# Two of the seven products of the gate and up units split once more, and the gate and up weight sums made in SBUF

## The chip, the cores and the metric

The kernel runs on one core of a Trainium2 chip. The metric is the device time of one execution in microseconds. The time of the kernel before is the median of three runs.

## What is computed

An RWKV layer at its first time step, followed by a gated feed-forward layer, on 2048 tokens of 512 features in float32. Only the second half is touched by the change:

```
x = x + rwkv(layernorm(x))            # time mix, channel mix: about the first 53% of the time
z = layernorm(x)
gate, up = split(z @ w_gate_up.T)     # 2048 x 512 times 512 x 4096
h = silu(gate) * up                   # 2048 x 2048
x = x + h @ w_down.T                  # 2048 x 2048 times 2048 x 512
```

## The kernel before

**Tiles.** The tokens are cut into 4 blocks (`b`) of 512. A weight of 512 x 512 is a "block" `n` of four quarters of 256 x 256: `WG + g` and `WU + g` are the four gate and four up blocks (`g` = 0 to 3).

**A unit** (`unit`, line 583) is one product of a weight block with a token block, 512 x 512 x 512, after Strassen and Winograd: seven products of quarters instead of eight. The weights' sums S1 to S4 and the activations' sums T1 to T4 are made ahead; the sums after the products are folded into the order of the accumulation. One product is 4 matmuls of 128 x 128 weights with 256 moving columns (L602). Its steps are `step1` (A11·B11, copied by ScalarE to the bank `accv`, L622), `step2` (A12·B21 on `accv`), `step6` (S2·T2, copied to `u2`, L633), `step5` (S1·T1, copied to `accx`, L637) and, put off into the next unit through the list `held`, `step7` (S3·T3), `step3` (S4·B22 on `accx`) and `step4` (A22·T4). `sink(i, j, c)` takes each finished quarter: `ffn_gate` (L1162) applies Silu on ScalarE, `ffn_up` (L1174) multiplies on VectorE (`tt`, L431).

**The down products** (`down_product`, L1273) already split a second time: seven products of 256 wide operands, each of seven products of 128 x 128 x 128 quarters over four chunks (L1342). ScalarE keeps intermediate results (`keep`, L1354).

**Weights.** The ring `wring` has 12 buffers of 256 KB. `weight` (L200) issues a load on SP's queue (L197) for each product, in the order of the products; a load waits until a buffer is released by the matmuls that used it. S1 to S4 come from a DRAM scratch: `prepare` (L172) loads four quarters on POOL's queue (L181), makes four sums on VectorE, and stores them (L192). The blocks to prepare stand in the lists `early` and `late` (L1456 to L1459); `tick` gives them turns by `credit`, and `need_sums` forces them when a product needs them.

**Order.** TensorE, VectorE and ScalarE each run in the order in which the Python code emits the instructions. A product is emitted, then `tick` (L339) emits VectorE work from the queues `hot` (`urgent`) and `background` (`push`) as far as an estimate of VectorE's time allows. An instruction that waits holds up everything behind it on its engine.

**PSUM.** Eight banks: `accv`, `accx`, and a pool `ps` of six.

**The feed-forward stage** (L1532 to L1551): for each block, gate 0, up 0, gate 1, up 1 and so on, then gate 0 of the next block, then the down product. `load_resid(b + 1)` (L1126), which asks for the residual (1 MB) and x (4 x 256 KB) of the next block on SP's queue, stands ahead of up 0. `ffn_in(b + 1)` (L1131: residual plus x, moments, normalisation, transposes, `sums_of`) is pushed to the background after up 1. Token tiles come from `tokp`, five buffers of 1 MB.

Of the kernel before, what the change touches and what calls it, by code (L numbers as in the profile page):

```python
# [9 lines left out]
F32 = mybir.dt.float32  # L10
AF = mybir.ActivationFunctionType
ALU = mybir.AluOpType
# [9 lines left out]
EPS = 1e-5  # L22
WAIT = 5
LONG = 6
STEP = 1.72
SHARE = 0.88
WARM = 24
# [36 lines left out]
def rwkv_ffn_kernel(  # L64
# [20 lines left out]
    up = ctx.enter_context(tc.tile_pool(name="up", bufs=10))  # L85
    prep = ctx.enter_context(tc.tile_pool(name="prep", bufs=6))
    small = ctx.enter_context(tc.tile_pool(name="small", bufs=3))
    ps = ctx.enter_context(tc.tile_pool(name="ps", bufs=6, space=bass.MemoryType.PSUM))
    pv = ctx.enter_context(tc.tile_pool(name="pv", bufs=1, space=bass.MemoryType.PSUM))
    px = ctx.enter_context(tc.tile_pool(name="px", bufs=1, space=bass.MemoryType.PSUM))  # L90
    dram = ctx.enter_context(tc.tile_pool(name="dram", bufs=1, space=bass.MemoryType.DRAM))


# [16 lines left out]
        return tokp.tile([P, NT, H], F32, tag="tok", name=name)  # L110

    def bank():
        return ps.tile([P, 2, HB], F32, tag="ps", name="ps")

# [29 lines left out]
    def value_part(q, k):  # L146

        if q < 4:
            return wv[q, k].rearrange("p (g c) -> p g c", c=P)
        m, kk = divmod((0, 1, 3, 2)[k], 2)  # L150
        return vsum[q - 4][:, :, kk, m * P : (m + 1) * P]

    for q in (A11, A12, A22, S1, S2, S3, S4):
        sources["vv", q] = [value_part(q, k) for k in range(4)]
# [40 lines left out]
    def ring(src):  # L195
        t = wring.tile([P, 2, HB], F32, tag="w", name="w")
        nc.sync.dma_start(flat(t), src)  # L197
        return t

    def weight(n, q):  # L200
        if q >= 4:
            need_sums(n)
            return ring(sums[n][q - 4])
        return ring(sources[n][q])

    def down_weight(q, k):

# [10 lines left out]
    def value_weight(q, k):  # L218

        if k >= 4:  # L220
            need_sums(("vv", q))
            return ring(sums["vv", q][k - 4]).rearrange("p a (h c) -> p (a h) c", c=P)
        if q >= 4:
            for g in range(4):
                need_sums(WVAL + g)
        t = wring.tile([P, 2, HB], F32, tag="w", name="w")
        t = t.rearrange("p a (h c) -> p (a h) c", c=P)
        nc.sync.dma_start(t, value_part(q, k))
        return t

    def load_x(b, queues=None):
        t = tok_tile("x")
# [58 lines left out]
    preps = deque()  # L291
    credit = [0.0, 0.0]
    pause = [WAIT]

    def prep_one():
        item = preps[0]
        if item[1] > 0:
            return False
        try:
            if next(item[2]) is not None:  # L300
                item[1] = pause[0]
        except StopIteration:
            preps.popleft()
            finished.add(("sums", item[0]))
            if len(preps) > 1 and item[3] > 1:
                begin(preps[1])
            elif preps:
                begin(preps[0])
        return True
# [7 lines left out]
    def prepare_all(ns, own, depth):  # L317
        empty = not preps
        for n in ns:
            preps.append([n, 0, prepare(n, own), depth, False])  # L320
        if empty:
            for item in list(preps)[:depth]:
                begin(item)
# [58 lines left out]
    nc.vector.memset(warm, 0.0)  # L382
    nc.scalar.activation(warm, warm, AF.Exp)

    pt = ps.tile([P, 2, HB], F32, tag="ps", name="warm")
    for _ in range(WARM):
        nc.tensor.transpose(pt[:, 0, 0:P], ident, ident)

# [194 lines left out]
    def unit(weights, Bs, sink, by_token, done=None, free=None):  # L583
# [86 lines left out]
        for s in order:  # L670
            if s is None:
                pop_held()
            else:
                s()
                tick()
        held.extend(((STEP, step7), (STEP, step3), (STEP, step4)))

    def plain_unit(n, B, sink, by_token, done=None, free=None, halfway=None, hold=False):

# [451 lines left out]
    def ffn_in(b):  # L1131
        r, xr = loads.pop(b)
        for t in range(NT):
            tt(r[:, t, :], r[:, t, :], xr[:, t, :], ALU.add)
            yield
        rs[b] = r
        mv = small.tile([P, NT, 2], F32, tag="mv", name="mv")
        yield from moments(r, mv)
        var = small.tile([P, NT], F32, tag="var", name="var")
        ts(var, mv[:, :, 1], EPS, None, ALU.add)  # L1140
        rstd = small.tile([P, NT], F32, tag="rstd", name="rstd")
        yield from rsqrt(var, rstd, NT)
        z = tok_tile("z")
        yield from scaled(r, z, mv, rstd)
        m, B = op_tile("zT")
        ops[b, "z"] = B
        yield 1

        def evacuate(c, pt):
            k = c // 2  # L1150
            nc.scalar.copy(
                m[:, 2 * k : 2 * k + 2, c % 2, :], pt.rearrange("p (j t) -> p j t", j=2)
            )

        yield from transposed(z, evacuate)
        finished.add((b, "z"))
        yield 1
        yield from sums_of(B)

    gated = {}  # L1160

    def ffn_gate(b, g):  # L1162
        s = gated[b, g] = {}

        tile_of = q_tile if g % 2 else u_tile

        def sink(i, j, c):
            t = tile_of("s")
            nc.scalar.activation(t, c, AF.Silu)
            s[i, j] = t  # L1170

        unit([WG + g], [Lazy((b, "z"))], sink, False)

    def ffn_up(b, g):  # L1174
        s = gated.pop((b, g))
        hid = hidden.setdefault(b, {})

        def sink(i, j, c):
            q = (B11, B12, B21, B22)[2 * i + j]
            if q not in hid:  # L1180
                hid[q] = hidden_tile()
            tt(hid[q][:, g], c, s[i, j], ALU.mult)
            if g == 3:
                made.add((b, q))
                if q in (B11, B22):
                    quarter_sums(b, 0 if q == B11 else 1)

        unit(
            [WU + g],
            [Lazy((b, "z"))],  # L1190
            sink,
            False,
            lambda: hidden_done(b, g),
            op_done if g == 3 else None,
        )

    def hidden_done(b, g):
        hid = hidden[b]
# [35 lines left out]

    def last_room():
        middle.close()
        pools["q"] = ctx.enter_context(
            tc.tile_pool(name="fq", bufs=4, reuse_waits="tile")
        )

    def quarters(t):
        return {2 * k + m: t[:, :, k, m * P : (m + 1) * P] for k in range(2) for m in range(2)}
# [212 lines left out]

    early = [WV, WCR, WO] + [WKEY + g for g in range(4)] + [WVAL, WVAL + 1]  # L1456
    late = [("vv", q) for q in (A11, S4, S2, A12, S1, S3, A22)]
    late += [n + g for g in range(4) for n in (WG, WU)] + [("dd", A11)]
    late += [("d", k) for k in range(4)] + [("dd", q) for q in (S4, S2, A12, S1, S3, A22)]  # L1459

    ctx.enter_context(
        tc.manual_schedule(
# [25 lines left out]
    for b in range(NB):  # L1488
# [3 lines left out]
        if b == NB - 1:  # L1492
            load_resid(0)
        if b >= DEEP:
            credit[1], pause[0] = 1.0, LONG
        gate_unit(b)
        if b + 1 < NB:
            out_unit(b + 1)
# [30 lines left out]
        if nxt:  # L1529
            for n, u in (("k", k_unit), ("r", r_unit), ("v", v_unit)):  # L1530
                u(b + 2)
    credit[1] = 0.75  # L1532
    need((0, "z"))
    ffn_gate(0, 0)
    last_room()
    for b in range(NB):
        for g in range(4):
            if g > 0:
                need((b, "z"))
                ffn_gate(b, g)  # L1540
            if g == 0 and b + 1 < NB:
                load_resid(b + 1)
            ffn_up(b, g)
            if g == 1 and b + 1 < NB:
                push((b + 1, "z", "t"), ffn_in(b + 1), op_free)
        if b + 1 < NB:
            need((b + 1, "z"))
            ffn_gate(b + 1, 0)
        ffn_down(b)
    release()  # L1550
    flush()  # L1551

# [77 lines left out]
```

## Time and profile before

| | |
|---|---|
| median of 3 runs | 1232.57 us (1230.68 to 1233.49) |
| the profiled execution | 1231.09 us, its span 1229.0 us |
| TensorE busy in the span | 1219.5 us |
| first feed-forward product to the end | about 655 to 1229 us |
| down products of the four blocks begin at | 770, 912, 1055, 1183 us |

Times in the profile count from the start of the span. PE is TensorE, PEld its weight loads, DVE VectorE, ACT ScalarE, SP the engine that issues most loads. A float32 matmul appears as two records, so a product of 4 matmuls has 8. In a list of groups the columns are line, engine, operation, names, shapes and count, then busy time with the mean of one, then the engine's idle time before them and who ended it.

### The profile page before, as it was taken

How to read it: one execution, taken by the hardware profiler on the slowest of the kernel's cores; microseconds unless marked ns; L12 is line 12 of the kernel's file. 1: busy time of each engine (PE TensorE's matmuls, PEld its weight loads, DVE VectorE, ACT ScalarE, POOL GpSimd, SP SyncE). 2: the span in 40 equal slices, each digit the busy share in tenths (PEclk: the TensorE clock that was granted, in tenths of full speed). 3: DMA queues.
4: the chain of work that ended last, by engine and by line, in shares of the span. 5: the costliest groups of instructions: out<-in, count | busy, mean ns of one | idle time of the engine just before them, and what ended most of it. 6: DMA issues, size and time to landing. Idle time of an engine off the chain costs nothing.

```text
span 1229.0 us, 19201 instructions
## 1 busy us (share of the span) xinstructions
PE 1219.5 (99%) x6860; PEld 1106.3 (90%) x6860; DVE 780.3 (63%) x1451; ACT 368.4 (30%) x713; POOL 186.6 (15%) x334
## 2 busy tenths in 40 slices
PE   9999999999999999999999999999999999999998
PEld 8888888888888888998899888998899888998898
DVE  5877686577685666886775577646546364553466
ACT  5534252242532333323412222112221232112211
POOL 2232221223212222002201222200000000000000
PEclk9999999999999999999999999999999999999999
DMA  5768985899888988899889978995469745785576
GB/s 196 250 221 282 319 299 206 302 320 302 277 262 270 312 288 263 261 297 381 280 281 329 335 232 279 362 343 154 146 194 309 258 143 153 250 290 154 153 225 204
DMA packets 159620, 319.03 MB, mean 260 GB/s; under 512 B 19096, under 2 KB 32552, under 8 KB 158248
## 3 DMA queue, kind: packets, MB, share of 16 engines
q1 hardware_dynamic: 132000, 230.22, 58.4%
q0 software_dynamic: 25920, 84.96, 19.0%
q10 hardware_dynamic: 1608, 2.65, 0.7%
q8 instruction: 55, 0.90, 0.3%
q14 instruction: 37, 0.30, 0.1%
HBM read 268.46 MB, written 49.29 MB: 259 GB/s over the span
## 4 chain that ended last, share of the span: by engine, by line
PE 90%; DVE 4%; DMA 3%; ACT 2%; issue 1%; POOL 1%; ACTq 0%; DVEq 0%; POOLq 0%
PE ps L602 45%; PE ps L1342 21%; PE accx L602 9%; PE accv L602 9%; PE ps L704 5%; DMA raw<-in_w 2%; PE ps L487 1%; DMA vsum<-raw 1%; DMA row<-stats 1%; ACT mix L540 1%; DVE raw L431 0%; DVE e L439 0%; DVE h L435 0%; DVE st L445 0%; POOL raw L181 0%
## 5 line engine op out<-in xcount | busy, mean ns | idle before, releaser
L602 PE MATMUL ps<-zT,w 128*128 128x256 f32 x1280 | 289.3, 380 | 0.0
L602 PEld LDWEIGHTS ps<-zT,w 128*128 128x128 f32 x1280 | 242.4, 191 | 31.5
L602 PE MATMUL ps<-mix,w 128*128 128x256 f32 x920 | 211.1, 380 | 1.3 <-ACT u L633 1.3
L602 PEld LDWEIGHTS ps<-mix,w 128*128 128x128 f32 x920 | 174.3, 190 | 24.5 <-ACT u L633 1.7
L1342 PE MATMUL ps<-w,hid 128*128 128x128 f32 x1248 | 156.8, 275 | 0.0
L1342 PEld LDWEIGHTS ps<-w,hid 128*128 128x128 f32 x1248 | 149.7, 192 | 1.2
L1342 PE MATMUL ps<-w,quads 128*128 128x128 f32 x1056 | 133.5, 276 | 0.4 <-ACT r L1354 0.4
L1342 PEld LDWEIGHTS ps<-w,quads 128*128 128x128 f32 x1056 | 126.4, 192 | 1.1 <-ACT r L1354 0.5
L1354 ACT COPY r<-ps 128x128 f32<-128x128 f32 x168 | 44.5, 265 | 204.5 <-PE ps L1342 201.9
L431 DVE TENSOR_TENSOR raw<-raw 128x512 f32<-128x512 f32 x120 | 82.5, 688 | 30.9 <-issue 11.1
L431 DVE TENSOR_TENSOR u<-u,accx 128x512 f32<-128x512 f32 x64 | 43.8, 685 | 85.7 <-ACT accx L637 85.7
L431 DVE TENSOR_TENSOR hid<-hid 128x512 f32<-128x512 f32 x126 | 84.9, 687 | 2.0 <-ACT hid L1068 0.3
L622 ACT COPY accv<-ps 128x512 f32<-128x512 f32 x64 | 36.5, 571 | 158.0 <-PE ps L602 155.2
L637 ACT COPY accx<-ps 128x512 f32<-128x512 f32 x64 | 36.5, 570 | 132.7 <-PE ps L602 126.2
L431 DVE TENSOR_TENSOR u<-ps,u 128x512 f32<-128x512 f32 x64 | 44.2, 690 | 44.5 <-PE ps L602 40.6
L704 PE MATMUL ps<-mix,w 128*128 128x256 f32 x320 | 70.8, 380 | 1.1 <-DVE mix L439 1.1
L633 ACT COPY u<-ps 128x512 f32<-128x512 f32 x64 | 37.4, 584 | 109.5 <-PE ps L602 109.5
L704 PEld LDWEIGHTS ps<-mix,w 128*128 128x128 f32 x320 | 60.4, 191 | 9.5 <-DVE mix L439 1.8
L431 DVE TENSOR_TENSOR r<-ps,r 128x256 f32<-128x256 f32 x83 | 29.8, 359 | 51.5 <-PE ps L1342 47.1
L602 PE MATMUL accv<-zT,w 128*128 128x256 f32 x256 | 60.6, 380 | 0.0
L602 PE MATMUL accx<-zT,w 128*128 128x256 f32 x256 | 60.5, 380 | 0.0
L602 PE MATMUL ps<-w,t 128*128 128x256 f32 x264 | 59.4, 379 | 0.0
(179 smaller groups left out, 1593.7 us busy)
## 6 DMA issues: line engine op xcount, KB each, us to landing
w<-sum SPq DMA_DIRECT2D x248, 256.0 KB, 4.2
w<-in_w SPq DMA_DIRECT2D x230, 256.0 KB, 4.2
w<-dd SPq DMA_DIRECT2D x112, 256.0 KB, 3.8
w<-vsum SPq DMA_DIRECT2D x56, 256.0 KB, 4.4
w<-vv SPq DMA_DIRECT2D x56, 256.0 KB, 4.0
raw<-in_w POOLq DMA_DIRECT2D x48, 256.0 KB, 6.7
w<-d SPq DMA_DIRECT2D x48, 256.0 KB, 3.5
sum<-raw POOLq DMA_DIRECT2D x40, 256.0 KB, 4.1
```

Of the source, the lines that this page charges most:

```text
L431: nc.vector.tensor_tensor(out, a, b, op)
L487: nc.tensor.transpose(flat[:, t * P : (t + 1) * P], h[:, t, c * P : (c + 1) * P], ident)
L540: nc.scalar.activation(dst(c), hT[:, c, 0:TB].rearrange("p (j t) -> p j t", j=2), AF.Copy, scale=onem[:, row - MK, c : c + 1],)
L602: mm = nc.tensor.matmul(pz[:, m, :], lhsT=lhsT, rhs=rhs, start=first and g == 0 and m == 0 and k == 0, stop=g == last and k == 1, skip_gro ...
L622: "z", A11, B11, True, pop_held, read=lambda: nc.scalar.copy(accv, acc["z"])
L633: nc.scalar.copy(tmp["u2"], acc["z"])
L637: nc.scalar.copy(accx, acc["z"])
L704: mm = nc.tensor.matmul(acc[i, j][:, m, :], lhsT=act[:, k, lo] if by_token else wg[:, k, lo], rhs=wg[:, k, :] if by_token else act[:, k, : ...
L1342: mm = nc.tensor.matmul(dst, lhsT=x[k][:, g, :], rhs=wt[:, g, :], start=first and g == 0, stop=g == 3, skip_group_check=True,)
L1354: nc.scalar.copy(st["r"][:, m, n * P : (n + 1) * P], st["z"])
```

## The change

**Split.** In the gate and up units from block 1 on (but gate 0 of block 1, which stays a `unit`, and up 0 of block 1, which is a `paired_unit` without a split), A11·B11 and S3·T3 are no longer 4 matmuls with 256 columns each. Both are split once more into seven products of 128 x 128 x 128, computed side by side (`i` = 0, 1) by `inner`, in five pieces that stand between the products of the unit before. The results go to one of two halves `r` of a token tile `pair` in SBUF. ScalarE later copies A11·B11 into the banks `z` and `accv`, on which the unit's products then accumulate; S3·T3 is added by VectorE in the sinks as `plus`. S3·T3, A11·B11 and their separate weight loads leave; the two raw weights stay, and two loads of their inner sums (`insums`, from DRAM) come: 9 loads of 256 KB for a unit instead of 7. The put off products become one (`last`, S4·B22) instead of three.

**PSUM.** After block 0 the six banks are given up for `z`, `w` and a pool of four (`pair_room`); before that `release()` runs all held steps.

**Weight sums.** Of the gate and up blocks only the first, `WG`, is still prepared ahead. For the other seven, `jit_load` puts the raw quarters into the weight ring one to two units early in block 0, `jit_sums` makes S1 to S4 and the inner sums on VectorE straight from them, the products of block 0 use these tiles, and POOL stores them for the later blocks. The blocks of the down weights are prepared in the place of these in the list; all that is left of them is forced before gate 0 of block 0. From block `DEEP` of the first half, `credit` is 0.65 instead of 1.0 and the next item begins earlier (`AHEAD`).

**Later requests.** `load_resid(b + 1)` now stands behind up 0, and `ffn_in(b + 1)` is pushed right after it.

```diff
 def weight(n, q):
+    if n in jit and (n, q) not in at_once:
+        at_once.add((n, q))
+        while q not in jit[n]:
+            run_one(True)
+        return jit[n][q]
...
+def jit_sums(n):
+    x = jit[n]
+    for o, i0, i1, op in (
+        (S1, A21, A22, ALU.add),
+        (S2, S1, A11, ALU.subtract),
+        (S3, A11, A21, ALU.subtract),
+        (S4, A12, S2, ALU.subtract),
+    ):
+        t = prep.tile([P, 2, HB], F32, tag="raw", name="raw")
+        tt(t, x[i0], x[i1], op)
+        x[o] = t
+        nc.gpsimd.dma_start(sums[n][o - S1], flat(t))
+        yield
+    for q in (A11, S3):
+        yield from small_sums(n, q, x[q])
...
+    def mm(dst, q, k, start):
+        for i in range(2):
+            m = nc.tensor.matmul(dst[:, i, :], lhsT=wt(i, q), rhs=act(i, k), ...)
+    def keep(m, j):
+        nc.scalar.copy(st["r"][:, :, m, j * P : (j + 1) * P], st["z"])
+    def one():
+        st["r"] = pair_tile()
+        st["w"] = [weight(n, A11), weight(n, S3)]
+        st["s"] = [inner_weight(n, A11), inner_weight(n, S3)]
...
+        mm(st["z"], A11, B11, True)
+        keep(0, 0)
+        mm(st["y"][:, :, 0, :], A12, B21, True)
+    def two():
+        mm(st["z"], S2, T2, False)
+        keep(1, 0)
+    def three():
+        mm(st["z"], S1, T1, False)
+        keep(0, 1)
+        mm(st["y"][:, :, 1, :], S4, B22, False)
+        later(joined, 1)
+    def joined():
+        r = st["r"]
+        tt(r[:, :, 1, :P], r[:, :, 1, :P], r[:, :, 0, P:], ALU.subtract)
+        tt(r[:, :, 0, :], st["y"]..., r[:, :, 0, :], ALU.add)
+    def four():
+        mm(st["z"], S3, "T3", False)
+        keep(1, 1)
+    def five():
+        mm(st["z"], A22, T4, False)
+        r = st["r"]
+        tt(r[:, :, 1, :P], st["z"], r[:, :, 1, :P], ALU.add)
...
+def paired_unit(at, b, n, after, sink, done=None, free=None):
...
+    z, aw = acc2["z"], acc2["w"]
+    plus = None if st is None else st["r"][:, 1]
+    small()
+    pop_held()
...
+    small()
+    product(z, S2, T2)
...
+        nc.scalar.copy(aw, z)
+    small()
+    product(accv, A12, B21)
+    sink(0, 0, accv)
...
+    small()
+    product(z, S1, T1)
+    nc.scalar.copy(accx, z)
+    sink(1, 1, z, plus)
+    small()
+    if after is not None:
+        r = ahead[after[0]][0]["r"][:, 0]
+        nc.scalar.copy(z, r)
+        nc.scalar.copy(accv, r)
+    product(aw, A22, T4, st is None)
+    end = sink(1, 0, aw, plus if u2 is None else u2)
...
+    def last():
+        product(accx, S4, B22)
+        sink(0, 1, accx)
...
-late += [n + g for g in range(4) for n in (WG, WU)] + [("dd", A11)]
-late += [("d", k) for k in range(4)] + [("dd", q) for q in (S4, S2, A12, S1, S3, A22)]
+late += [WG, ("dd", A11)]
+late += [("d", k) for k in range(4)] + [("dd", q) for q in (A12, S4, S2, S1, S3, A22)]
...
-            credit[1], pause[0] = 1.0, LONG
+            credit[1], pause[0], AHEAD[0] = CREDIT, LONG, 2
...
+    while preps:
+        need_sums(preps[-1][0])
     ffn_gate(0, 0)
     last_room()
     for b in range(NB):
         for g in range(4):
             if g > 0:
                 need((b, "z"))
                 ffn_gate(b, g)
+            ffn_up(b, g)
             if g == 0 and b + 1 < NB:
                 load_resid(b + 1)
-            ffn_up(b, g)
-            if g == 1 and b + 1 < NB:
                 push((b + 1, "z", "t"), ffn_in(b + 1), op_free)
         if b + 1 < NB:
             need((b + 1, "z"))
             ffn_gate(b + 1, 0)
         ffn_down(b)
+        if b == 0:
+            pair_room()
```

The five calls of `small()` run `one` to `five` of the next unit's split; `pop_held()` runs `last` of the unit before.

## The prediction

> **What bounds the kernel now.** I read the page's busy shares first, then who waited for whom, then the chain, then each stage.
>
> ```profile
> span 1229.0 us, 19201 instructions
> PE 1219.5 (99%) x6860; PEld 1106.3 (90%) x6860; DVE 780.3 (63%) x1451; ACT 368.4 (30%) x713; POOL 186.6 (15%) x334
> ```
>
> TensorE misses 9.5 us of the span: 2.6 of them before the eleventh microsecond, 4.4 in the last eight. From 549 us to the end the view of waits has one line for it:
>
> ```profile
> PE ps L1342 <- ACT r L1354: 0.4, 1, 0.4
> ```
>
> So in the feed-forward stage nothing but the number and length of matmuls counts. A microsecond of matmuls removed is a microsecond gained; a microsecond in which TensorE is made to wait is lost in full, since no slack stands beside it. The chain gives the prices (start, length, records):
>
> ```profile
> 509.81 39.31 PE ps L1342 x352
> ...
> 566.52 6.91 PE ps L602 x32
> ```
>
> 256 columns: 6.91/32 = 0.216 us a record, 0.432 a matmul, 1.727 a product. 128 columns: 39.31/352 = 0.1117, 0.223 a matmul, 0.893 for four.
>
> **What the split saves.** Of the 32 gate and up units, 8 of block 0 and two of block 1 keep all seven products; 22 are split. Each loses two products, 3.454 us, and gains 14 matmuls of 128 columns, 3.127 us: 0.328 us, in 22 units **-7.2 us**. The order of the built program agrees: 176 fewer of the long matmuls, 308 more of the short. All the rest of the change can only be free or cost.
>
> [...]
>
> **Rows of an ordinary feed-forward stretch and of the down product** (length, then busy time of PE, PEld, DVE, ACT, POOL, then clock, DMA share, GB/s):
>
> ```profile
> 844.00:856.00 12.00, 12.00 (x57) 10.58 (x57) 9.80 (x29) 2.87 (x5) 0.00 (x0) 1.00 0.53 152
> ...
> 912.00:952.00 40.00, 40.00 (x357) 39.92 (x356) 24.97 (x48) 7.12 (x26) 2.12 (x3) 1.00 0.90 295
> ```
>
> **Loads.** A split unit is 12.09 - 0.33 = 11.76 us long and asks for 9 x 256 KB, 201 GB/s. The down product runs without a wait at 295. In the built order the shortest way from release of a ring buffer to use is 7.4 us of matmuls, against 2.6 us to landing in quiet feed-forward stretches (median, 820 to 912 us) and 3.5 at the last down product. Taken at nothing; if loads landed in 7.9, the worst median I found (660 to 685 us), each unit would wait 0.5.
>
> **The single banks.** `z` is copied, refilled and read in turn. After S1·T1 comes: copy to `accx` 0.57 (L622's and L637's rows), VectorE's add and product 0.69 + 0.69, `five`'s add 0.43, two copies of `r` into banks, `keep` of the next `one` about 0.37 (between 0.27 and 0.57). TensorE must have the last of these before `two`, and has `five`, A22·T4, `one` and `last` to do first: 0.45 + 1.73 + 0.89 + 1.73 = 4.79 us. With 0.57 for the copies into banks (no row shows ScalarE writing there) the chain is 3.9. Even at 0.81, the dearest row of ScalarE for this size, it is 4.4. Taken at nothing, in either direction. But it has under a microsecond of margin, and VectorE's queue is in it.
>
> **The later requests: the dear part.** In `before` the loads for block 2 go out at 809.57 and 809.98 and are read at 843.13:
>
> ```profile
> 809.57 0.32 SPq L1128 DMA_DIRECT2D resid<-res  x1
> 809.98 2.16 SPq L235 DMA_DIRECT2D x<-in_x  x4
> ```
>
> ```profile
> 843.13 1.88 DVE L431 TENSOR_TENSOR resid<-resid,x 128x512 f32<-128x512 f32 x3
> ```
>
> Landing took 6.3 us for the residual and for x:
>
> ```profile
> DMA to landing us min/median/max: 7.6/7.8/7.8
> ```
>
> That is 8.1 us after the first request, hidden under 33. In the changed program the requests wait for up 0's A22·T4, and behind that product's own add and multiplication VectorE's next instruction is `ffn_in`'s first add. VectorE has nothing else by about 2 us later, stops there, and with it all that is queued behind: the product of `last`, four hidden sums, `joined`, the (1,1) add, `five`'s add. Only then can ScalarE fill `z` and do `keep`, for which TensorE's `two` waits. From the landing of x on I count: four residual adds 4 x 0.63 (1.88/3), the product 0.69, four sums 2.7, `joined` 0.42 + 0.69, (1,1) 0.69, a moment's pair 0.8, `five` 0.43: 8.9; ScalarE's two copies and keep 1.5, steps between engines 0.1: 10.5. TensorE has, from the request to the next unit's `two`, six long products (`last`, S2·T2, A12·B21, S1·T1, A22·T4, `last`: 10.4), three pieces of four short matmuls (`one`, `three`, `one`: 2.7) and three of two (`two`, `four`, `five`: 1.3): 14.4 us. So it waits for landing - 3.9. Landing: above, 8.1 by the row; below, a quiet load's 2.6 plus 1 MB at the 395 GB/s of a full stretch, 2.65, plus 0.4 until x is issued: 5.6. I take 7.0, nearer the row, since three weight loads go out in the 2 us before: 3.1 us for block 2. For block 3 x also waits for block 1's last store, some 0.4 us more: 3.5. **+6.6 us** (3.4 to 9.2). For block 1 the requests come 14 us ahead of the add: nothing.
>
> [...]
>
> **Other places, each worked out from the built order.**
> - *End of block 0's down product.* `release()` puts the last two pieces of it back to back, each waiting for a keep as in the 0.4 us line above, and S2·T2 of up 0 has only `two` over the copy to `accv`: 0.35 + 0.35 + 0.2, **+0.9** (0.4 to 1.5).
> - *Last up unit of blocks 1 and 2.* Four quarter sums (2.7) stand on VectorE between the (0,0) product and the (1,1) add, which makes the chain above some 0.4 late each: **+0.8** (0 to 2).
> - *Transposes with four banks.* The third set waits for ScalarE's 0.6 us copy of the first: 0.25 in two blocks, **+0.5** (0 to 1).
> - *Start of the stage.* Raw blocks go ahead of gate 0's weights in SP's queue; S1 of gate 0 has 4.35 us of matmuls from release to use, against landings of 3.7 to 4.1 there: **+0.5** (0 to 1.5).
> - *Sums in SBUF.* Per unit of block 0 VectorE gets 4 x 0.69 + 8 x 0.29 = 5.1 us, and loses 7.5 preparations of 2.75 that `before` has there. Its 65 of the 105 us (664 to 769) become about 85. The sums are due one unit later, and block 0 still has six banks: 0. With small collisions elsewhere **+0.3** (0 to 2). The lists of the first half hold as many items up to 611 us as before (12 against 11.5), and TensorE waits for none of them: 0, from -0.5 to +0.5.
>
> **The sum.** -7.2 + 6.6 + 0.9 + 0.8 + 0.5 + 0.5 + 0.3 = +2.4. On the profiled execution's 1231.09 (span 1229.0 and 2.1 around it) that makes **1233.5 us**. This execution lies 1.5 below the median of 1232.57 and within the runs; I leave the number there. With all low ends: -7.2 + 3.8 - 0.5, 1227; with all high ends +10.5, 1241.5.
>
> **Rivals.**
> - *The waits stay small.* Landing at 5.6 or less and VectorE catching up: 1231.1 - 7.2 + 2.5 = 1226.5. For it: a quiet DMA (152 GB/s) in these blocks. Against: 1 MB of residual comes first, and nothing of VectorE's queue can pass the add. Chance 0.26.
> - *Slower by over 0.2%.* The same blocked add, with x landing at 8.1 us or later: 4.2 and 5.0 us of waits, and VectorE, which then still owes moments and normalisation (some 6 us), makes the next unit wait another 1.2 in both blocks: 11.6 instead of 6.6, about 1238.5. It decides from a landing of about 7.1 us, where the sum passes +2.5. Chance 0.28.
> - *The bank chain does not fit at all.* A wait of 0.4 in each of 22 units: 1242. Against: the margin above. Chance 0.06.
> - *The split saves nothing* is excluded by the counts; that block 0's sums hold TensorE up instead would show as waits between 664 and 769 us, and is in the 0.3.
>
> **How the numbers follow.** The forecast's case, saving and waits about equal, has 0.40 and lies between 1230 and 1236. About 0.2% is what a measurement of this kernel can tell from no change, 2.5 us. Faster: 0.26. Within: 0.30 of the forecast's case and 0.02 of the next. Slower: 0.10 + 0.26 + 0.06 = 0.42. The range from 1226 to 1241 reaches over both ends of the unknown costs and most of the first rival. Cases of both signs hold most of the chance; the forecast's own is 1230 to 1236.
>
> **What would show it.** Split units 11.8 us apart in block 3; VectorE idle for about 5 us before `resid<-resid,x`, released by DMA, early in gate 1 of blocks 1 and 2, and TensorE waiting for ScalarE's `pair` copy some 14 us after the requests; about 0.7 us at the end of block 0's down product. Wrong if x is there when VectorE arrives, if TensorE waits in units of block 3, or if it waits in block 0.

## The result and the profile after

The changed kernel takes 1248.74 us (median of 4 runs, 1245.89 to 1252.59), the kernel before 1232.84 (four runs): a ratio of 1.0134, with an interval of 1.0103 to 1.0166. It is slower by 1.3%, and the time lies outside the predicted 1226 to 1241. Its runs also lie further apart (6.7 us, against 2.8 before). The profiled execution is the longest of the four, 1252.59 us; what follows accounts for its span, 21.8 us over the span before.

TensorE's line of its page (span 1250.8 us):

```profile
PE 1222.4 (98%) x7124; PEld 1108.8 (89%) x7124; DVE 827.0 (66%) x1594; ACT 407.5 (33%) x824; POOL 180.3 (14%) x322
```

So TensorE misses 28.4 us of the span, not 9.5. And though the split took 7.2 us of matmul out, its busy time rose by 2.9: some matmuls took longer. The mean granted clock says the same: 0.995, where before it was 1.000.

Who waited for whom, TensorE alone, from 549 us to the end (total, times, longest). Before, this answer had one line of 0.4 us:

```profile
PE ps L798 <- ACT pair L809: 8.7, 4, 4.1
PE accx L682 <- DVE u L511: 3.9, 1, 3.9
PE ps L682 <- ACT accx L717: 2.6, 3, 1.2
PE ps L1693 <- ACT r L1705: 1.1, 3, 0.4
```

First the saving. Two neighbouring units of block 3, TensorE's rows of the timeline:

```profile
1157.45 1.89 PE L881 MATMUL accx<-zT,w 128*128 128x256 f32 x8
...
1169.21 1.89 PE L881 MATMUL accx<-zT,w 128*128 128x256 f32 x8
```

They start 11.76 us apart, against 12.09 before: 0.33 a unit, as predicted, with no wait between.

Then the blocked add, in the timeline of block 1 (requests for block 2):

```profile
839.75 0.33 SPq L1399 DMA_DIRECT2D resid<-res  x1
...
840.16 3.27 SPq L311 DMA_DIRECT2D x<-in_x  x4
...
848.31 1.29 DVE L511 TENSOR_TENSOR resid<-resid,x 128x512 f32<-128x512 f32 x2 [7.06 <-DMA x<-in_x]
...
858.46 0.71 PE L798 MATMUL ps<-inner,w 128*128 128x128 f32 x4 [4.14 <-ACT pair L809]
...
859.01 3.40 PE L881 MATMUL accz<-zT,w 128*128 128x256 f32 x8
```

VectorE stands for 7.06 us until x lands, 8.56 us after the first request; TensorE waits 4.14 us for the `pair` copy behind it. The last row is what nobody had priced: the product behind the wait takes 3.40 us, not 1.89. Two neighbouring windows of 3.41 us, the first with most of the wait in it (length; busy time of PE, PEld, DVE, ACT, POOL; then the clock, DMA share, GB/s):

```profile
855.82:859.23 3.41, 0.77 (x5) 0.74 (x6) 3.31 (x9) 2.86 (x6) 0.00 (x0) 1.00 0.21 69
859.23:862.64 3.41, 3.41 (x11) 2.78 (x9) 2.91 (x15) 0.59 (x3) 0.00 (x0) 0.50 0.00 0
```

The granted clock was halved for 3.41 us behind the wait, which costs 1.7 us more of matmul time. This happened three times: behind the waits of 3.90, 4.14 and 3.87 us.

The 3.90 us stand where the feed-forward stage begins, in block 0:

```profile
679.95 0.33 SPq L1399 DMA_DIRECT2D resid<-res  x1
...
680.33 2.51 SPq L311 DMA_DIRECT2D x<-in_x  x4
...
681.08 0.54 POOL L305 DMA_DIRECT2D in<-pair  x1 [0.39 <-DVE pair L511]
...
689.45 0.29 DVE L511 TENSOR_TENSOR pair<-w 128x128 f32<-128x128 f32 x1 [8.67 <-DMA in<-pair]
...
...
690.72 2.60 PE L682 MATMUL accx<-zT,raw 128*128 128x256 f32 x8 [3.90 <-DVE u L511]
```

Read it upwards: TensorE waits for VectorE's `u`, VectorE had been stopped at `pair<-w`, and that waits for a store. The store of gate 1's S3 sums reads row 3 of `pair`; gate 0's own S3 sums, made after it, are to be written to the same row. It landed 8.4 us after its issue (the median of these 16 stores is 4.4). Of the 2 MB of residual and x, 1.5 had gone out in the 1.1 us before it, the rest in the 1.2 us after.

The account of the 21.8 us. Losses are distances between the starts of neighbouring matmuls less the usual 0.216 or 0.112, so they hold the 0.16 us too that each of the 15 waits from 549 us on costs beyond its length (at 858.46: 4.515 us from start to start, 4.136 of them idle, 0.216 usual):

| | predicted | profiled execution |
|---|---|---|
| split, 22 units | -7.2 | -7.2 |
| blocked add, blocks 2 and 3 | +6.6 | +8.5 |
| half clock behind it, 2 x 1.7 | none | +3.4 |
| store wait at the entrance, half clock behind it | none | +4.2 +1.7 |
| waits for `accx` in block 0 | 0 | +3.4 |
| first half of the kernel | 0 | +3.3 |
| start of the stage | +0.5 | +0.8 |
| end of block 0's down product | +0.9 | +1.4 |
| last up units, quarter sums | +0.8 | +1.3 |
| transposes with four banks | +0.5 | +0.8 |
| sum (the prediction's has 0.3 for small collisions too) | +2.4 | +21.6 |

### The profile page after: what moved, and what is told of

Read it like the earlier page. It is cut to its first block, busy times and chain, and to the rows that moved or that the text cites. A ratio compares the mean times of both kernels' runs of the same rounds, so it can differ in the third digit from the quotient of the medians.

```text
span 1250.8 us, 20032 instructions
## 1 busy us (share of the span) xinstructions
PE 1222.4 (98%) x7124; PEld 1108.8 (89%) x7124; DVE 827.0 (66%) x1594; ACT 407.5 (33%) x824; POOL 180.3 (14%) x322
## 4 chain that ended last, share of the span: by engine, by line
PE 77%; DVE 8%; DMA 7%; issue 4%; ACT 2%; POOL 1%; ACTq 0%; POOLq 0%; DVEq 0%
PE ps L682 23%; PE ps L1693 20%; PE accz L881 6%; PE accx L682 5%; PE ps L798 5%; PE accv L682 5%; PE ps L975 4%; PE accv L881 3%; PE accw L881 2%; PE accx L881 2%; DMA x<-in_x 2%; DVE hid L511 1%; PE ps L567 1%; DMA raw<-in_w 1%; DMA raw<-d 1%
## 5 line engine op out<-in xcount | busy, mean ns | idle before, releaser
L881 PE MATMUL accz<-zT,w 128*128 128x256 f32 x376 | 91.8, 388 | 0.0
L511 DVE TENSOR_TENSOR raw<-raw 128x512 f32<-128x512 f32 x92 | 63.2, 686 | 39.8 <-issue 22.0
L881 PEld LDWEIGHTS accz<-zT,w 128*128 128x128 f32 x376 | 69.5, 195 | 8.0
L798 PEld LDWEIGHTS ps<-inner,w 128*128 128x128 f32 x352 | 53.2, 194 | 15.2 <-ACT pair L809 10.3
L511 DVE TENSOR_TENSOR r<-r 128x128 f32<-128x128 f32 (+1 forms) x83 | 40.3, 486 | 36.3 <-ACT r L1705 34.9
L798 PE MATMUL ps<-inner,w 128*128 128x128 f32 x352 | 54.6, 278 | 8.8 <-ACT pair L809 8.7
L1789 POOL DMA_DIRECT2D out<-resid x12 | 8.6, 715 | 370.4 <-DVE resid L511 351.6
L511 DVE TENSOR_TENSOR quads<-hid,quads 128x512 f32<-128x512 f32 x84 | 57.7, 687 | 1.4
L682 PEld LDWEIGHTS ps<-w,t 128*128 128x128 f32 x264 | 50.1, 190 | 6.8
L717 ACT COPY accx<-ps 128x512 f32<-128x512 f32 x41 | 23.4, 571 | 94.6 <-PE ps L682 72.8
```

The costliest lines, as they stand in the source:

```text
L511: nc.vector.tensor_tensor(out, a, b, op)
L682: mm = nc.tensor.matmul(pz[:, m, :], lhsT=lhsT, rhs=rhs, start=first and g == 0 and m == 0 and k == 0, stop=g == last and k == 1, skip_gro ...
L717: nc.scalar.copy(accx, acc["z"])
L798: m = nc.tensor.matmul(dst[:, i, :], lhsT=wt(i, q), rhs=act(i, k), start=start and i == 0, stop=True, skip_group_check=True,)
L881: mm = nc.tensor.matmul(dst[:, m, :], lhsT=wg[:, kk, m * P : (m + 1) * P], rhs=act[:, kk, :], start=start and m == 0 and kk == 0, stop=kk ...
L1789: eng.dma_start(out_t[b][:, tokens, cols], rs[b][:, tokens, cols])
```

## The experiments

**The two large losses, one at a time.** The requests of blocks 1 and 2 ahead of up 0:

```
+            if g == 0 and b + 1 < NB and b > 0:
+                load_resid(b + 1)
             ffn_up(b, g)
             if g == 0 and b + 1 < NB:
-                load_resid(b + 1)
+                if not (b > 0):
+                    load_resid(b + 1)
                 push((b + 1, "z", "t"), ffn_in(b + 1), op_free)
```

> The changed kernel with one move: in blocks 1 and 2 the residual and x of the next block are asked for ahead of up unit 0 again, not behind it (about 13 us of matmuls earlier); ffn_in still joins VectorE's queue behind up 0, and block 0 is left alone. Theory A (the add that waits for x holds VectorE, and a TensorE wait of about 4 us is followed by 3.4 us at half clock, 1.7 us more): both waits of `two` for ScalarE's `pair` copy (4.1 and 3.9 us) and the half-clock stretches behind them go, x is there when VectorE comes to the add; 4.1 + 3.9 + 2 x 1.7 = 11.4 us less than the changed kernel, about 1237. Rival B (the waits come from the mass of ffn_in's work that follows at once, moments and all, not from the landing): VectorE no longer stops, but `two` still waits 1 to 3 us in each block; 4 to 7 us less, 1242 to 1245. Rival C (the half clock is not tied to the waits): the waits go and the half-clock stretches stay; 8 us less, 1240.7.

Measured: 1241.36 us (ratio to before 1.0077, 1.0059 to 1.0094), 7.4 less than the changed kernel; by the profiled executions 10.4 less. TensorE's waits (two lines of the list):

```profile
PE accx L682 <- DVE u L511: 3.9, 1, 3.9
...
PE accx L881 <- DMA w<-sum: 1.0, 1, 1.0
```

Both `pair` waits of some 4 us and the half clock behind them are gone, and x is there when VectorE comes to the add: of the three theories, A holds. But the median gains 7.4 where A had 11.4. 1.0 us came back as a wait for weights behind the early 2 MB; the rest is not explained. The changed kernel's other three runs are 2.7 to 6.7 us shorter than its profiled one, and two of them have the same mean clock of 0.995, so the clock alone is not the reason. The entrance is untouched.

The other row at the entrance:

```
         k = (n < WU) * 2 + (q == S3)
+        if n == WG:
+            k = 2 - (q == S3)
```

> The changed kernel with one row changed: the sums of gate 0's S3 are written to row 1 of the tile in place of row 3, which the store of gate 1's S3 sums still reads (8.4 us from its issue to its landing). Theory A: the 8.7 us in which VectorE waited for that store go, and with them the 3.9 us in which TensorE waited for `u` in S4 of gate 0's neighbour and the half clock behind it: 3.9 + 0.3 + 1.7 = 5.9 us less than the changed kernel, about 1242.8. Rival B: row 1 has its own store in flight (up 0's) or the ring buffers hold VectorE next; then the wait moves and less than 2 us is gained, 1247 or more.

Measured: 1242.42 us (1.0086, 1.0065 to 1.0106), 6.3 less. The store still takes up to 8.6 us to land, but nobody waits for it:

```profile
PE ps L800 <- ACT pair L811: 7.3, 4, 3.7
PE ps L684 <- ACT accx L719: 2.6, 3, 1.2
```

(Lines lie two further on, by the edit.) So one row, to be written while a store still read it, cost 6 us.

The same early requests in block 0 alone (the edit of the first run with `b == 0`):

> The changed kernel with the requests for block 1's residual and x ahead of up unit 0 of block 0 again (some 12 us of matmuls earlier), all else as changed. If the store of 681 us was late because 2 MB of residual and x had been asked for in the microsecond before it, it lands in about 4 us (the median of these stores is 4.4), VectorE waits 8.7 - 4.3 = 4.4 us instead of 8.7, TensorE nearly not, and its clock stays whole: 4 to 6 us less than the changed kernel, 1243 to 1245. Rival: the store is late for other reasons (the eight raw loads of the same stretch): it still lands in 8 us and nothing changes, 1248.

Measured: 1256.67 us (1.0190, 1.0167 to 1.0214), 8 us slower. Both theories fell. Timeline:

```profile
667.65 0.33 SPq L1399 DMA_DIRECT2D resid<-res  x1
...
668.07 2.00 SPq L311 DMA_DIRECT2D x<-in_x  x4
...
671.23 0.33 SPq L1385 DMA_DIRECT2D res<-x  x1
...
672.28 0.38 SPq L206 DMA_DIRECT2D w<-sum  x1
...
684.80 3.57 PE L682 MATMUL accx<-zT,w 128*128 128x256 f32 x8 [10.27 <-DMA w<-sum]
```

Two MB of loads and a store of 1 MB go out ahead of the one 256 KB load that gate 0's S4 product needs; that load is used 12.5 us after its issue. So in block 0 the requests are not to go ahead of up 0. Behind up 1:

```
-            if g == 0 and b + 1 < NB:
+            if g == (b == 0) and b + 1 < NB:
                 load_resid(b + 1)
```

> The changed kernel with block 1's requests and its ffn_in one unit pair later in block 0 (behind up 1, not up 0), all else as changed. The move ahead of up 0 made it slower, since the load of gate 0's S4 sum then stood behind 3 MB and landed 12 us after its issue. If mass in the queues is the cause in the changed kernel too, the store of gate 1's S3 sums at 681 us now lands in about 4.4 us, not 8.4: VectorE waits some 4 us less, TensorE's 3.9 us wait in gate 0 / up 0 shrinks below 1 and its clock stays whole: 4 to 5.9 us less than the changed kernel, 1243 to 1245. Rival: the raw loads and the 1 MB store of the first half's last result at 671 us are mass enough: the store still lands in about 8 us, and the time stays at 1247 to 1249, or the 2 MB hurt one unit later instead.

Measured: 1245.42 us (1.0117, 1.0093 to 1.0140), 3.3 less; the store lands in 4.4 us, VectorE still waits for it, 4.7 us and not 8.7, and TensorE's 3.9 us at the entrance are gone. The 2 MB were about half of VectorE's wait. Some came back: block 1's transposes waited 2.2 us for the later `z`.

**The half clock.** Twelve idle matmuls in the wait, first into the unused half of the bank that is waited for, then with zeros into the unit's other bank:

```
         def two():
+            if n == WG + 2 and 0 < b < NB - 1:
+                for _ in range(12):
+                    nc.tensor.matmul(st["f"][:, HB : HB + P], lhsT=ident, rhs=ident, ...)
```

> The changed kernel with 12 idle matmuls more (128 columns, 0.223 us each, 2.7 us, into the unused half of a bank) put just ahead of the matmul that waits some 4 us for the `pair` copy in blocks 1 and 2. They fill the wait and add nothing to the result. If an idle TensorE of 3.4 us or more is what halves the clock afterwards: waits of 1.2 to 1.4 us, no half clock behind them, 2 x 1.7 = 3.4 us less than the changed kernel although there is more work, about 1245. If the half clock has another cause: no gain, 1248 to 1249; and if the waits were shorter than 2.7 us, slower.

Measured: 1255.51 us (1.0180, 1.0151 to 1.0209). It told nothing of the clock, for the filler waited itself, in its bank for the copy out of the other half, and took twice as long behind the wait, 0.229 us a record (5.49/24; 0.118 in the second try):

```profile
855.85 5.49 PE L826 MATMUL ps<-ident 128*128 128x128 f32 x24 [4.17 <-ACT pair L809]
```

The second try (`st["y"][:, 0, 1, :]`, `rhs=zeros`):

> The filler again, so placed that it waits for nothing: 12 matmuls with zeros (128 columns, 2.7 us) onto the other bank of the same split unit, ahead of the matmul that waits for the `pair` copy in blocks 1 and 2; they add zero. In the first try the filler itself had waited for that copy, so it told nothing of the clock. If it is the idle TensorE that halves the clock: idle time of 1.2 to 1.4 us in place of 3.9 and 4.1, the clock whole in blocks 1 and 2, and 3.4 us less than the changed kernel with more work, about 1245.3. If the half clock comes from the stall in another way (the engines around it, the load of the queues): it stays, 1248.7 or more.

Measured: 1245.73 us (1.0103, 1.0088 to 1.0118): 3.0 less than the changed kernel, with 5.4 us more work.

```profile
853.86 2.84 PE L827 MATMUL ps<-zeros,ident 128*128 128x128 f32 x24
856.87 0.71 PE L800 MATMUL ps<-inner,w 128*128 128x128 f32 x4 [0.17 <-ACT pair L811]
857.42 1.89 PE L886 MATMUL accz<-zT,w 128*128 128x256 f32 x8
```

The product behind takes 1.89 us, not 3.40, and the clock is 1.00 there (840 to 864 us). All four runs have a mean clock of 0.998, where three of the four of the changed kernel have 0.995. Two stretches of 3.41 us at half clock are 0.003 of the span, so by the mean two of the three are gone, and the entrance still has its wait (4.1 us). That fits the idle TensorE as the cause, but this profile alone does not show it: x landed earlier here (VectorE stood 5.5 us, not 7.1), and without the filler the wait would have been some 3.0 us (2.84 + 0.17). A wait of 2.9 us passed without a half clock in the run with block 1's requests behind up 1: the mean clock of its profiled execution is 1.000. The last section has TensorE's idle time ahead of each half clock.

**The first half, and sums made ahead.** The pacing of before:

```
-CREDIT = 0.65
+CREDIT = 1.0
...
-            credit[1], pause[0], AHEAD[0] = CREDIT, LONG, 2
+            credit[1], pause[0], AHEAD[0] = CREDIT, LONG, 9
```

(and the order S4, S2, A12 in the list of `dd`)

> The changed kernel with the pacing of the preparations as before (a credit of 1.0 in the deep blocks, the next item begun only when one ends, the old order of the down weights' list); the gate and up sums stay out of the list. It prices the 3.4 us by which the feed-forward stage begins later in the changed kernel (transposes for block 0: 590.5 and 594.5 us). Theory A (the new pacing makes VectorE late for small waits of TensorE): 2 to 3.4 us less, 1245.3 to 1246.7. Rival B (the list without the gate and up sums is what shifts the work, or it is the spread of executions): less than 1 us, 1248. Rival C (the list no longer ends in time): preparations are forced ahead of the feed-forward stage and hold it up, slower, 1250 or more.

Measured: 1247.22 us (1.0116, 1.0099 to 1.0133). The medians alone don't settle 1.5 us; the profiled executions of all runs together do: with the new pacing the feed-forward stage begins 0.8 to 4.1 us later than in `before` (mean 2.8 of nine), with the old 0.2 earlier to 2.2 later (mean 0.9 of eight; both counted from the same matmul at 97 us). The pacing, with the order of the list, costs some 1.8 us there. It reaches into block 0 too, where it changes what VectorE does when. The three waits for `accx` last 0.25, 0.45 and 0.45 us in this run (and the same in two later profiles with the old pacing, of 1233.36 and 1236.77 us below), against 0.45, 1.25 and 0.93 in the changed kernel:

```profile
PE ps L682 <- ACT accx L717: 1.2, 3, 0.5
```

So the profiles make the pacing worth some 3 us, where the median here gained 1.5; the difference is not explained.

Sums made ahead, no `jit`:

```
     def begin_jit(n):
+        return
...
-        if n == WG and q in (A11, S3) and (n, q) not in at_once:
+        if WG <= n < WU + 4 and q in (A11, S3) and (n, q) not in at_once:
...
-    late += [WG, ("dd", A11)]
+    late += [n + g for g in range(4) for n in (WG, WU)] + [("dd", A11)]
```

(with the pacing of before, and none of the list forced ahead of the stage)

> The split kept, the sums of the gate and up weights made as before (in the list of preparations, through DRAM, with the pacing of before); only the small sums of the two split products are made in SBUF in block 0, from the weights that each unit has there anyway. Requests stay where the change put them. Theory A (sums made at once put VectorE's orders in the way of the units of block 0): the entrance's 3.9 us and its half clock (1.7), the three waits for `accx` (2.6 with 0.7 of refilling) and 1.5 us of the first half go: 10.7 us less than the changed kernel, about 1238. Rival B (VectorE is simply full in block 0, and 8 small sums a unit beside the preparations do the same): no more than the 1.5 us of the first half, 1247. Rival C (preparations that end late hold up their loads in block 0): 1250 or more.

> As the run with the sums made ahead, with the requests for the next block ahead of up 0 in all three blocks, as before the change. If both repairs add up: 7.4 (measured) to 11.4 us less than the run beside it, about 1228 to 1231, faster than the kernel before by 0.1 to 0.3%: the split's 7.2 us less some 3.5 us that its own small waits cost (end of block 0's down product, quarter sums, transposes, pacing). If the collision of the entrance comes back (3 MB ahead of gate 0's S4 sum): 5 to 10 us more, 1236 or above. If the split itself costs what it saves: 1232 to 1235.

Measured: 1245.45 us (1.0108, 1.0088 to 1.0129) and, with early requests in all blocks, 1236.74 (1.0045, 1.0028 to 1.0062). The entrance is mended, but the losses come at another place: the down weights, last in the list, are now late at block 0's down product. In the second of these runs:

```profile
PE ps L1694 <- DMA w<-dd: 1.5, 2, 0.8
```

In the first, the two waits for `dd` came to 0.8 us, and for a third of 2.3 us there the profile shows no releaser. So sums made ahead are no free repair, and the sums in SBUF have their use: they keep this list short.

**Adding up.** Early requests in blocks 1 and 2 with the other row; then the old pacing too:

> The changed kernel with both repairs that gained by themselves: the requests for blocks 2 and 3 ahead of up 0 (7.4 us by itself) and the other row for the sums of gate 0's S3 (6.3 us). If they are two separate losses they add up: 1248.7 - 13.7 = 1235.0. If they share one (the half clock, or the queue behind the requests): 1238 or more.

> The run beside it with the pacing of the first half as before the change too. By itself that gave 1.5 us, within what the runs spread: 1233.5 if it is real, 1235 if it was spread.

Measured: 1234.54 us (1.0016, 1.0004 to 1.0028; expected 1235.0) and 1233.36 (1.0004, 0.9992 to 1.0017; expected 1233.5). The two losses are separate and add up. What is left, in the second:

```profile
PE accx L883 <- DMA w<-sum: 2.2, 1, 2.2
PE ps L684 <- ACT accx L719: 1.1, 3, 0.5
```

The first is a load of weights behind the early 2 MB in block 2 (0.8 us in the run beside it), the second the waits for `accx` in block 0. One of these, as the changed kernel has it:

```profile
721.06 0.69 DVE L511 TENSOR_TENSOR raw<-w,raw 128x512 f32<-128x512 f32 x1 [0.44 <-PE ps L682]
721.67 0.28 DVE L511 TENSOR_TENSOR pair<-w 128x128 f32<-128x128 f32 x1
...
724.35 0.66 DVE L511 TENSOR_TENSOR hid<-accx,s 128x512 f32<-128x512 f32 x1
...
725.10 0.57 ACT L717 COPY accx<-ps 128x512 f32<-128x512 f32 x1 [6.91 <-DVE hid L511]
...
725.72 1.99 PE L682 MATMUL ps<-zT,raw 128*128 128x256 f32 x8 [1.25 <-ACT accx L717]
```

VectorE frees `accx` behind the small sums, and those behind a sum that had waited for TensorE. First suspect, the small sums' place:

```
-        for q in (A11, S3):
-            yield from small_sums(n, q, x[q])
         finished.add(("sums", n))
+        later(lambda: urgent(("small", n), small_both(n, x)), 2)
```

> The two repairs, and the eight small sums of a unit of block 0 put off by two products, so that VectorE's product that frees `accx` stands ahead of them and not behind (in the changed kernel it came 1.2 us late, and TensorE waited 0.45, 1.25 and 0.93 us for the next copy to `accx`, and some 0.2 more each to fill its pipeline again). If VectorE's order is the cause: 3.3 us less than with the two repairs alone, about 1231.7. If VectorE is simply full there, the waits move to the next product: no gain, 1235.

> All of it: both repairs, the small sums put off, the first half paced as before. If the gains add up, 1248.7 - 7.4 - 6.3 - 1.5 - 3.3 = 1230.2: what is left of the split's 7.2 us then lies 1.5 us under the kernel before, since 3.5 us of its own small waits (end of block 0's down product, quarter sums, transposes) and about 2 of the first half stay. If the small sums gain nothing: 1233.5.

Measured: 1245.49 us (1.0097, 1.0074 to 1.0121) and 1241.76 (1.0061, 1.0044 to 1.0078), both slower. In the first, the three waits stayed (0.99, 0.97, 0.81 us; `ffn_in`'s add, statistics and normalisation now stood ahead of the product), and the new order brought the store wait of the entrance back: VectorE 7.6, TensorE 5.3 us. The small sums' place was not the cause; and the other row was a repair for one order of instructions only.

Second suspect, buffers, and the other half of the x repair (`ffn_in` queued behind up 1):

```
-            if g == 0 and b + 1 < NB and b > 0:
-                load_resid(b + 1)
             ffn_up(b, g)
             if g == 0 and b + 1 < NB:
-                if not (b > 0):
-                    load_resid(b + 1)
+                load_resid(b + 1)
+            if g == (b > 0) and b + 1 < NB:
                 push((b + 1, "z", "t"), ffn_in(b + 1), op_free)
...
-    prep = ctx.enter_context(tc.tile_pool(name="prep", bufs=6))
+    prep = ctx.enter_context(tc.tile_pool(name="prep", bufs=7))
```

> The best version so far (two repairs and the first half paced as before, 1233.4) with the other half of the x repair: the requests for blocks 2 and 3 stay behind up 0, where the change put them, and ffn_in joins the queue behind up 1 (some 24 us later), not behind up 0. If the blocked add is a matter of distance between request and add alone: no wait for x, as with the early requests, and also none of the 0.8 to 2.2 us in which TensorE waited for a load of weights behind these 2 MB in block 2: 1 to 2 us less, 1231.4 to 1232.4. If the late ffn_in makes the next block's transposes or the last units of the block late: 1234 or more.

> The best version so far with 7 buffers in place of 6 for the sums that VectorE makes (there is room for one more). In block 0 VectorE begins each of the next unit's sums when TensorE has read the buffer that it takes (12 waits, 14.1 us), so it moves in step with TensorE and frees `accx` late whatever stands behind, small sums or statistics. If that is the cause of the 0.25, 0.45 and 0.45 us in block 0 and the refilling behind them: 1 to 1.8 us less, about 1232. If VectorE is late for its own work: no change, 1233.4.

> Both at once: 1233.4 less 1 to 2 less 1 to 1.8, 1229.6 to 1231.4 if both gain; that would be the first version under the kernel before (1232.5), by 0.1 to 0.2%. If neither gains, 1233.4.

Measured: the later add 1236.77 us (1.0032, 1.0018 to 1.0045), slower by 3.4 than without; seven buffers 1230.58 (0.9984, 0.9974 to 0.9994); both 1235.28 (1.0028, 1.0018 to 1.0038). The later add brings a wait of its own, in both blocks:

```profile
894.13 0.94 PE L800 MATMUL ps<-zT,w 128*128 128x128 f32 x6 [2.44 <-DVE zT L513]
```

The small products of the next block's gate 0 run one unit ahead and read the sums of `zT` there. That needs `z` a unit earlier, so the add can't simply go back to where it was; it is the request that had to be early.

Seven buffers loosen the lock step. VectorE's waits from 655 to 785 us, with six and with seven:

```profile
DVE raw L513 <- PE ps L684: 14.1, 12, 2.5
```

```profile
DVE raw L513 <- PE ps L684: 7.1, 5, 2.2
```

With seven, TensorE's waits from 640 us to the end have no line for `accx` of block 0:

```profile
PE ps L1695 <- ACT r L1707: 1.1, 3, 0.4
PE accx L883 <- ACT pair L811: 0.9, 1, 0.9
PE ps L684 <- DMA w<-sum: 0.9, 1, 0.9
PE ps L800 <- ACT pair L811: 0.7, 2, 0.4
PE ps L569 <- ACT zT L1424: 0.5, 2, 0.2
```

This version is faster than the kernel before by 0.16%, and the only one that is.

## Why the prediction was wrong, step by step

- **The split**, -7.2: right to the hundredth (11.76 us a unit). So the short matmuls did cost 0.223 us. The loads and the single banks, costed at nothing: right, the units of block 3 have no wait at all.
- **The later requests**, +6.6: the mechanism was right, place and chain too. "It waits for landing - 3.9" gives 4.7 for the measured 8.56 us; the wait was 4.14. Two sizes were off. The landing was taken as 7.0 "nearer the row", and the row, 8.1, was the better guide: there as here, three weight loads had gone out in the 3 us ahead. And the price of a wait was taken as its length: the half clock behind it adds 1.7. Together 11.9 in place of 6.6. The rival "slower by the blocked add" had 11.6 for it, though for another reason, VectorE in arrears; its condition, a landing above 7.1, was met. (The second wait in it, 5.0, should have been 4.6 by the prediction's own 8.1 - 3.9 + 0.4.) The signs named for the blocked add were there: VectorE idle (7.06 and 6.55 us, not 5) ahead of the add, and TensorE stopping 14.6 us after the requests (839.75 to 854.3).
- **For block 1 "the requests come 14 us ahead of the add: nothing"**: the add indeed found its x, but the 2 MB held up what was under way beside them. A transfer was asked only who waits for it, not what it delays.
- **Sums in SBUF**, +0.3, is the step that failed outright: 9.3 us with the half clock, 5.9 at the entrance and 3.4 for `accx`. The prediction had named the sign: wrong "if it waits in block 0". It compared VectorE's work with its time (85 of 105 us). There was time enough (VectorE was busy for 73 of the 105 us from 667 us); the order was the limit. A write to a row that a store still read stopped VectorE for 8.7 us; changing the row gained 6.3. Of the waits for `accx`, 1.5 of 2.6 us come with the new pacing. The other 1.1 are gone with a seventh buffer, in both runs that have it: six held VectorE in step with TensorE. The two buffer questions (who reads this row, when does this buffer come free) were put to the weight ring and the banks, not to the `pair` rows and the `prep` pool.
- **The first half**, 0 +- 0.5: wrong by some 3 us, about 1.8 of them from the pacing and the list's order, which by the waits cost 1.5 more in block 0. The count of preparations was the same, but their place among VectorE's work moved, and TensorE's small waits for ScalarE and VectorE grew there.
- **Small places** (down product, quarter sums, transposes, start): all four were there; 2.7 predicted, 4.3 measured, in part since each wait of 0.24 to 0.36 us also costs 0.16 us beyond its length (six such waits).
- The range ended where all its high ends together end, at 1241.5. What lies beyond is the half clock, which had no term (5.1 us in three places), the sums in SBUF, whose bound was 2, and the first half, whose bound was 0.5.

What stays open: why the pacing makes the first half later was not followed to single waits. And seven buffers act on the first half too; the 2.8 us between the medians with six and seven are not split by place. The waits for `accx`, 1.1 us of idle time, are gone, but so is the 2.2 us wait for weights of the profiled execution with six, which the seventh buffer need not explain. Why one kernel's runs differ by up to 6.7 us was not followed either.

## What to carry to other kernels

Before a product is made cheaper on an engine that never waits, list for every added tile who still reads it when it is written again, stores above all; spare engine time says nothing about that. A load moved to a busy place is to be priced by what stands behind it in the queues as well as by who waits for it. A wait of TensorE can cost more than its length: in the changed kernel's profile the waits of 3.87, 3.90 and 4.14 us cost 1.7 us more each, by the half clock behind them. Those of 1.25 us and less did not, and in other runs some of 2.4, 2.9 and 3.91 us did not either.

## What the runs showed of the hardware

In the changed kernel's profile, past its first 20 us and ahead of its last 10, the granted clock falls to 0.50 three times, each time for 3.41 us, from 691.97, 859.23 and 1006.00 us: behind the waits of 3.90, 4.14 and 3.87 us. The other waits are 1.25 us long at most, and behind them it stays at 1.00. So it does in the profile before, where the longest is 1.29. Other runs have waits of a length between. Two of 2.4 us (the later add) and one of 2.9 us (block 1's requests behind up 1) passed in executions with a mean clock of 1.000, where one stretch at half clock would have taken 0.0014 off it. One of 3.91 us passed in the run with the pacing of before, so the 3.4 us of idle time that the first filler's expectation names is no bound.

The length of a wait does not decide alone. The three starts lie 167.25 and 146.77 us apart, 49 and 43 times 3.413 us, the length of the stretches themselves. Cut into windows at these times (without the three at half clock), the same part of the profile has 353 of them. The three with 2.16, 2.37 and 2.64 us without a matmul were followed by half clock; the other 350, with 1.74 us at most, were not. The third is 855.82 to 859.23 above; the first two, and the one with 1.74 us (PE's busy time is the number behind the length):

```profile
685.15:688.56 3.41, 1.67 (x8) 1.14 (x6) 0.00 (x0) 0.00 (x0) 0.00 (x0) 1.00 1.03 363
688.56:691.97 3.41, 1.25 (x6) 1.12 (x7) 2.48 (x7) 0.67 (x2) 0.01 (x1) 1.00 0.87 320
691.97:695.38 3.41, 3.41 (x10) 2.50 (x9) 2.19 (x4) 0.92 (x2) 2.15 (x4) 0.50 0.81 260
...
1002.59:1006.00 3.41, 1.04 (x7) 0.99 (x8) 3.31 (x9) 2.86 (x7) 0.00 (x0) 1.00 0.24 59
1006.00:1009.41 3.41, 3.41 (x12) 2.85 (x11) 2.91 (x16) 0.76 (x2) 0.00 (x0) 0.50 0.00 0
```

This is one execution; that the idle time in such a window decides is a reading of it, and not shown for other lengths. At the entrance TensorE waited for VectorE, in blocks 1 and 2 for ScalarE. Behind the 10.27 us in which it waited for a load, in the run with block 0's early requests, the next product took 3.57 us, and the one after it 1.89. The wait of 3.91 us in the run with the pacing of before is cut by the windows below into 1.98 and 1.93 us, and the clock stays at 1.00:

```profile
998.43:1001.84 3.41, 1.43 (x7) 0.92 (x5) 3.27 (x8) 0.63 (x1) 0.00 (x0) 1.00 0.83 279
1001.84:1005.25 3.41, 1.48 (x9) 1.38 (x10) 3.28 (x9) 2.69 (x6) 0.00 (x0) 1.00 0.10 32
1005.25:1008.67 3.42, 3.42 (x22) 3.11 (x20) 2.98 (x15) 0.86 (x2) 0.00 (x0) 1.00 0.31 77
```

The changed kernel's 3.90 us at the entrance were cut into 1.74 and 2.16, and the half clock followed.

A 256 KB load that is used 12.5 us after its issue, when 3 MB had gone out in the 4.6 us before it, was the other surprise: in the changed kernel, without the requests ahead of it, the same load landed in 4.9 us, and the median of the 220 loads of its kind is 4.2.
